# Values of two quads in one run, and their first moves issued from another queue: a cross-attention kernel on one core

## The chip, the core and the metric

One core of a Trainium2 chip. It has TensorE (PE, matmuls; its weight loads are shown as PEld), VectorE (DVE), ScalarE (ACT), GpSimd (POOL) and SyncE (SP, which here only issues DMAs). All run their own instructions in order and meet through semaphores. The metric is device time in microseconds: 567.95 is the median of three runs before the change (567.91 to 568.03).

## The reference, cut to what matters

Eight batches, each of 256 query rows `x` and 256 context rows `ctx`, 1024 wide, 32 heads of 32, all in float32:

```python
xn   = layernorm(x) * ln_gamma + ln_beta
Q    = split_heads(xn @ Wq.T)              # 8 x 32 heads x 256 x 32
K = V = split_heads(ctx)
S    = einsum('bhsd,bhtd->bhst', Q, K) * 32 ** -0.5
P    = softmax(where(mask, S, -inf))
attn = merge_heads(einsum('bhst,bhtd->bhsd', P, V))
out  = x + attn @ Wout.T
```

## The kernel before

**Quads and slots.** Four heads make a quad; a batch has NQ = 8 quads, so N = 64 quads in all. The main loop at the end of the kernel writes one slot for each `n` from 0 to 63. In a slot PE gets, in this order: `scores(n + 1)` (L486), output steps of place 0, `values(n - 2)` (L636), output steps of place 1, one query product of a coming batch (`query_product`, L447, in seven of eight slots), and, after the softmax has been written, output steps of place 2 (`product_steps`, L720). The other engines get `softmax(n + 1)` in the same slot. The order of every engine is this program order; no scheduler changes it, and semaphores are placed by what is read and written. Slots are named below by n modulo 8, slot 0 to slot 7 of a batch.

**Scores** of a quad are four heads side by side, each on 32 of PE's rows; their PSUM tiles `sc` have four buffers. **Values** work on tiles of 64 rows by 32 columns: 32 matmuls of the source, 64 records in the profile, into two PSUM tiles `pv` with two buffers. `copy_at` (ACT, L649) takes them to `at`. It is written inside the next softmax, after the first head's exponentials, so `pv` is free again well before the next values.

**Softmax** of a quad, head by head: DVE adds the mask and takes the minimum (L524), ACT takes the exponential with its sum (L528), DVE the reciprocal (`rden`, L535), POOL scales (L543), DVE transposes in blocks of 32 x 32 (L549) into `pT`, and ACT copies the second half of each pair of heads aside into `pc` (`aside`, L555). On ACT there are so eight exponentials, the first copy aside, copies of a query product (L457) in some slots, and the second copy aside, the last piece of a slot. Two of eight slots have on ACT after that a normalization of rows of `x` (L248), for slots 2 and 3. On DVE, additions of query products (L463 in slot 0, L468 in slots 5 and 6) stand between the third and the fourth transpose.

**Moves.** The blocks have to change partitions before values can read them. The tail of a quad's softmax does it with four DMAs of 128 KB, all on SP's queue: two first moves from `pT` to `pT` (L614), the loads of the slot (keys, values, rows of `x`), and two second moves from `pc` to `pT` (L618), which overwrite what the first moves have read and so wait for their landing. `values(n - 2)` reads a quad's `pT` three slots after its scores were written.

**Query products** of the next batch are seven products of quarter size (a Strassen scheme, S1, S4, A11, S2, S3, A22, A12 in slots 2 to 7 and 0), all in one PSUM bank; each one's result must be taken out before the next is begun or added to. The scores of the next batch begin in slot 7; their second half reads what S3's addition (L468, slot 6) leaves in `qa`. **Output products** are 28 steps (two records each) for each batch, spread over the slots of the next by the table `STEPS`, whose triples are the steps of places 0, 1 and 2.

Of the kernel before, what the change touches and what calls it, by code (L numbers as in the profile page):

```python
# [46 lines left out]
F32 = mybir.dt.float32  # L47
# [4 lines left out]
P = 128  # L52
# [7 lines left out]
def xattn_kernel(  # L60
# [10 lines left out]
    nc = tc.nc  # L71
# [4 lines left out]
    NQ = NC  # L76
    NH = P // HD
    NS = S // P
    NT = T // P
    NO = D // 512  # L80
    K = 32
# [4 lines left out]
    N = B * NQ  # L86
# [16 lines left out]
    ps_v = ctx.enter_context(tc.tile_pool(name="ps_v", bufs=2, space=PS))  # L103
# [367 lines left out]
    mbs, scs, pTs, pvs, ats, pos = {}, {}, {}, {}, {}, {}  # L471
# [19 lines left out]
    def softmax(*args):  # L491
        for _ in softmax_parts(*args):
            pass
# [2 lines left out]
    BY_ACT = range(1, 2 * NQ)  # L496
    BY_DVE = range(NQ, 2 * NQ)


    def softmax_parts(n, copies=(), ahead=(), between=(), hooks={}, fill=()):  # L500

        fill = list(fill)

        def fill_in():
            if fill:
                fill.pop(0)()  # L510

        pss = scs[n]
        pT = pTs[n] = ptp.tile([P, 2, NI, NH, NS, K], F32, tag="pT", name=f"pT_{n}")
        pc = asp.tile([P, NI, NH, NS, K], F32, tag="pc", name=f"pc_{n}")
        es, mns, dens = {}, {}, {}

        def exps(j, part=range(NS)):
            if 0 in part:
                es[j] = ep.tile([P, NS, T], F32, tag="e", name=f"e_{n}_{j}")
                mns[j] = sm.tile([P, NS], F32, tag="mn", name=f"mn_{n}_{j}")  # L520
                dens[j] = sm.tile([P, NS], F32, tag="den", name=f"den_{n}_{j}")
            e, mn, den = es[j], mns[j], dens[j]
            for s in part:
                nc.vector.tensor_tensor_reduce(  # L524
                    out=e[:, s, :], in0=pss[j][:, s, :], in1=mbs[n // NQ], scale=1.0,
                    scalar=NO_SCORE, op0=ALU.add, op1=ALU.min, accum_out=mn[:, s : s + 1],
                )
                nc.scalar.activation(  # L528
                    e[:, s, :], e[:, s, :], AF.Exp, bias=mn[:, s : s + 1], scale=-1.0,
                    accum_out=den[:, s : s + 1],  # L530
                )

        def normalize(j):
            rden = sm.tile([P, NS], F32, tag="rden", name=f"rden_{n}_{j}")
            nc.vector.reciprocal(rden, dens[j])  # L535
            for s in range(NS):
                if j == NH - 1 and n in BY_ACT:
                    nc.scalar.activation(
                        es[j][:, s, :], es[j][:, s, :], AF.Copy, scale=rden[:, s : s + 1]
                    )  # L540
                    continue
                engine = nc.vector if j == 1 and n in BY_DVE else nc.gpsimd
                engine.tensor_scalar(  # L543
                    es[j][:, s, :], es[j][:, s, :], rden[:, s : s + 1], 1.0,
                    ALU.mult, ALU.mult,
                )

        def blocks(j):
            nc.vector.transpose(  # L549
                pT[:, :, :, j, :, :].rearrange("p a i s k -> p (a i) s k"),  # L550
                es[j].rearrange("p s (b t) -> p b s t", t=K),
            )

        def aside(j):
            nc.scalar.copy(pc[:, :, ts(j, 2)], pT[:, 1, :, ts(j, 2)])  # L555

        if n == 0:
            for j in range(NH - 1):
                exps(j, (0,))
            yield  # L560
            exps(NH - 1, (0,))
            fill_in()
            yield
            for j in range(NH):
                exps(j, (1,))
            normalize(0)
            fill_in()
        else:
            exps(0)
            while tails:  # L570
                tails.pop()()
            for done in list(pvs):
                copy_at(done)
            exps(1)
            for hook in hooks.get("soon", ()):
                hook()
            exps(2)
            normalize(0)
            exps(3)
        if n <= NQ + 1:  # L580
            for copy in copies:
                copy()
        for hook in hooks.get(0, ()):
            hook()
        normalize(1)
        fill_in()
        if n in BY_DVE:
            normalize(2)
        blocks(0)
        for hook in hooks.get(1, ()):  # L590
            hook()
        if n not in BY_DVE:
            normalize(2)
        fill_in()
        if n in BY_ACT:
            normalize(3)
        blocks(1)
        aside(0)
        if n not in BY_ACT:
            normalize(3)  # L600
        fill_in()
        blocks(2)
        while fill:
            fill_in()
        if n > NQ + 1:
            for copy in copies:
                copy()

        def tail():
            blocks(3)  # L610
            aside(1)

            for r in range(2):
                nc.sync.dma_start(pT[ts(2 * r, K), 1], pT[ts(2 * r + 1, K), 0])  # L614
            for load in between:
                load()
            for r in range(2):
                nc.sync.dma_start(pT[ts(2 * r + 1, K), 0], pc[ts(2 * r, K)])  # L618

        for load in ahead:  # L620
            load()
        if n < NQ or n > N - NQ:
            tails.append(tail)
        else:
            tail()
        yield

    def values(n):
        pvs[n] = [
            ps_v.tile([P, 2, NS, K], F32, tag="pv", name=f"pv_{n}_{r}") for r in range(2)  # L630
        ]
        pT = pTs.pop(n)
        for i in range(NI):
            for j in range(NH):
                for r in range(2):
                    nc.tensor.matmul(  # L636
                        pvs[n][r][j * HD : (j + 1) * HD],
                        vs[n - n % 2][ts(r, 2 * K), i, ds(n % 2 * P + j * HD, HD)],
                        pT[ts(r, 2 * K), :, i, j, :, :],
                        start=(i == 0), stop=(i == NI - 1),  # L640
                    )

    def copy_at(n):
        b, c = divmod(n, NQ)
        k, c = divmod(c, NK)
        if c == 0:
            ats[b, k] = atp.tile([P, NK, NS, NA, K], F32, tag="at", name=f"at_{b}_{k}")
        for r, pv in enumerate(pvs.pop(n)):
            nc.scalar.copy(  # L649
                ats[b, k][:, c, :, ts(r, 2), :], pv.rearrange("p a s k -> p s a k")  # L650
            )
# [16 lines left out]
    P1_ASIDE = (0, 1, 2, 3, 4, 5)  # L668
    STEPS = ((0, 0, 0), (0, 7, 0), (0, 1, 2), (0, 2, 2), (0, 2, 1), (0, 1, 2), (0, 0, 3), (0, 1, 2),
             (0, 2, 0))  # L670
    ENDS = ((0, 0, 2), (0, 0, 5), (0, 0, 5)) + ((0, 0, 4),) * 4 + ((0, 0, 0),)
    ENDS_TO = {2: (0, 0), 3: (0, 1), 4: (1, 1), 5: (1, 0), 6: (1, 1), 7: (0, 1)}

    def steps_of(b):
        if b == B - 2:
            return ENDS
        return STEPS

    assert all(sum(map(sum, steps_of(b))) == len(PRODUCTS) * NK for b in range(B - 1))

    def operand(b, name):
# [237 lines left out]
    for b in range(B - 1):  # L919
        done, ends = 0, b == B - 2  # L920
        for i, counts in enumerate(steps_of(b)):
            n = NQ * (b + 1) + i
            for place, k in enumerate(counts):
                steps.setdefault((n, place), []).append((b, range(done, done + k)))
                done += k
        for i, *what in (
            ((2, keep_p1), (3, take_po_q), *((i, copy_po, i) for i in range(3, 8))) if ends else
            ((1, keep_p1), *(((2, add_p1, 0, 0),) if b else ()), (2, store, 0, 0), (3, take, 0, 1), (4, take, 1, 1), (6, store, 1, 0),
             (7, store, 1, 1), (8, store, 0, 1))
        ):  # L930
            evacuations[NQ * (b + 1) + i].append((what[0], b, *what[1:]))
# [6 lines left out]
    for n in range(N):  # L938
        b, i = divmod(n - NQ, NQ)
        new_q = new_qs[n]  # L940
        between = []
# [5 lines left out]
        if n + 3 in firsts or n + 2 in firsts:  # L947
            between, ahead = between + ahead, []
# [18 lines left out]
        for what, one, *args in evacuations[n]:  # L967
            if one == B - 2:
                now.append(partial(what, one, *args))
            else:  # L970
                place = 0 if i in (3, 4, 6) or i < 3 and what is not add_p1 else "soon" if i == 2 else 1
                hooks.setdefault(place, []).append(partial(what, one, *args))
        if n >= 2:
            values(n - 2)
        project_steps(n, 1)
        copies = [partial(copy_q, q) for q in new_q]
# [105 lines left out]
    for c in range(2):  # L1082
        end_steps(to_c11, "A12", B21, (c,), (0,))
        end_steps(to_c21, "A22", T4, (c,), (0,))
    values(N - 2)
    copy_at(N - 2)
    end_sum(slice(2, 3), nc.gpsimd)
# [3 lines left out]
    s2t2 = ps_o.tile([P, 512], F32, tag="po", name="po_end_s2")  # L1091
    end_steps(s2t2, "S2", T2, range(2), (0,))
    values(N - 1)
    copy_at(N - 1)
    end_sum(slice(3, 4), nc.vector)
# [67 lines left out]
```

## Time and profile before

| what | before |
|---|---|
| median of three runs | 567.95 us (567.91 to 568.03) |
| span of the profiled execution | 566.0 us |
| around the span, to the median | 1.95 us |
| PE busy | 561.4 us, 99% |
| DVE, ACT, POOL busy | 467.6, 423.4, 394.3 us |
| granted TensorE clock | 1.000 over the span |
| eight slots from 292.31 us on | 67.93 us |
| DMA | 119.02 MB, 210 GB/s in the mean |

The time of the profiled execution is known only by its span, from first to last instruction; the runs' times hold a little more around it. A row of the order of time gives start and length in microseconds, engine and line, what is written and read, and how many equal instructions follow each other; a bracket behind it is idle time of that engine just before and what ended it. Rows of SPq and ACTq are DMA issues of these engines' sequencers. PE's matmuls overlap, so a run's length reaches over the next one's start; start to start is what it costs.

### The profile page before, as it was taken

The numbers are of one execution on the slowest core, as the hardware profiler recorded it, in microseconds if no ns is written. First come the engines' busy times: TensorE is split into PE (matmuls) and PEld (weight loads), VectorE is DVE, ScalarE is ACT, GpSimd is POOL, SyncE is SP. The second block draws the span as 40 slices with busy tenths as digits, with TensorE's granted clock in tenths as the row PEclk, the third lists the DMA queues.
The fourth block names the chain that finished last, engine by engine and source line by source line (L and its number), as shares of the span: only waits on it lengthen the run. The fifth ranks groups of instructions, "written<-read, shape, count | busy, mean of one in ns | idle before, by whom it ended". The sixth has DMA issues, their size and how long they took to land.

```text
span 566.0 us, 20200 instructions
## 1 busy us (share of the span) xinstructions
PE 561.4 (99%) x7266; PEld 393.7 (70%) x7266; DVE 467.6 (83%) x1716; ACT 423.4 (75%) x1464; POOL 394.3 (70%) x636
## 2 busy tenths in 40 slices
PE   8999999999999999999999999999999999999997
PEld 8788886767766767667766776667766767755454
DVE  5889889999988988878898888988888777879923
ACT  4699999997778866786777876778776776769820
POOL 2788887899777656857568665777648657448780
PEclk9999999999999999999999999999999999999999
DMA  8966667856697777966778767796658864536751
GB/s 310 397 181 199 185 198 228 281 162 179 212 301 232 223 202 235 263 195 191 233 216 239 215 176 221 230 273 193 176 140 269 255 191 128 146 110 180 218 156 74
DMA packets 47219, 119.02 MB, mean 210 GB/s; under 512 B 8976, under 2 KB 9744, under 8 KB 47120
## 3 DMA queue, kind: packets, MB, share of 16 engines
q1 hardware_dynamic: 46976, 117.74, 69.5%
q8 instruction: 57, 0.93, 0.8%
q14 instruction: 42, 0.34, 0.2%
q10 hardware_dynamic: 144, 0.01, 0.0%
HBM read 66.33 MB, written 11.53 MB: 138 GB/s over the span
## 4 chain that ended last, share of the span: by engine, by line
PE 97%; DMA 1%; DVE 0%; POOL 0%; ACT 0%; issue 0%; SPq 0%; POOLq 0%
PE po_S L720 21%; PE pq_A L447 19%; PE pv L636 12%; PE sc L486 12%; PE po_A L720 11%; PE pq L345 9%; PE pq_S L447 8%; PE po_end L787 3%; PE po_last L787 1%; DMA x<-in_x_dram 1%; PE po_end_s L787 0%; POOL x L885 0%; PE pq L290 0%; PE px L307 0%; ACT e L528 0%; PE px L273 0%
## 5 line engine op out<-in xcount | busy, mean ns | idle before, releaser
L543 POOL TENSOR_SCALAR e<-e,rden 128x256 f32<-128x256 f32 x466 | 215.4, 479 | 125.5 <-DVE rden L535 123.0
L528 ACT ACTIVATE e<-e,mn 128x256 f32<-128x256 f32 x512 | 254.0, 502 | 46.1 <-DVE mn L524 44.9
L549 DVE STREAM_TRANSPOSE pT<-e 128x512 f32<-128x512 f32 x256 | 178.9, 703 | 35.6 <-POOL e L543 27.5
L524 DVE CUSTOM_DVE_ANT_0 e<-sc,mb 128x256 f32<-128x256 f32 x512 | 185.3, 415 | 25.4 <-PE sc L486 25.1
L555 ACT COPY pc<-pT 128x512 f32<-128x512 f32 x128 | 79.0, 617 | 55.7 <-DVE pT L549 35.6
L528 ACT ACTIVATION_READ_ACCUMULATOR e<-e,mn 128x1 f32 x512 | 98.4, 192 | 0.0
L486 PEld LDWEIGHTS sc<-k,qa 32*128 32x128 f32 x1024 | 46.1, 184 | 42.2 <-issue 21.6
L720 PE MATMUL po_S<-wo,at 128*128 128x512 f32 x152 | 74.3, 606 | 0.0
L636 PE MATMUL pv<-pT,v 64*32 64x128 f32 x4096 | 74.1, 274 | 0.0
L486 PE MATMUL sc<-k,qa 32*128 32x256 f32 x1024 | 73.6, 401 | 0.1
L636 PEld LDWEIGHTS pv<-pT,v 64*32 64x32 f32 x4096 | 57.0, 105 | 22.5 <-issue 11.8
L720 PE MATMUL po_A<-wo,at 128*128 128x512 f32 x128 | 59.4, 605 | 0.0
L345 PE MATMUL pq<-xnT,wq 128*128 128x256 f32 (+1 forms) x240 | 55.0, 384 | 0.0
L447 PEld LDWEIGHTS pq_A<-xnT,wq 128*128 128x128 f32 x416 | 48.5, 192 | 6.2 <-issue 4.8
L345 PEld LDWEIGHTS pq<-xnT,wq 128*128 128x128 f32 x240 | 44.6, 190 | 8.2 <-issue 1.5
L720 PE MATMUL po_S<-wo,s 128*128 128x512 f32 x104 | 50.1, 606 | 0.0
L447 PE MATMUL pq_A<-xnT,wq 128*128 128x128 f32 x416 | 48.5, 275 | 0.0
L535 DVE RECIPROCAL rden<-den 128x2 f32<-128x2 f32 x256 | 38.2, 150 | 7.3 <-ACT e L528 6.2
L524 DVE DVE_READ_ACCUMULATOR2_ANT mn<- 128x1 f32 x512 | 42.4, 83 | 0.0
L720 PEld LDWEIGHTS po_A<-wo,at 128*128 128x128 f32 x128 | 22.9, 189 | 25.6 <-issue 24.5
L720 PEld LDWEIGHTS po_S<-wo,at 128*128 128x128 f32 x152 | 25.5, 190 | 19.5 <-issue 19.5
L753 POOL TENSOR_TENSOR r<-r,p 128x512 f32<-128x512 f32 x24 | 30.6, 1277 | 4.8 <-ACT e L528 3.0
(102 smaller groups left out, 666.1 us busy)
## 6 DMA issues: line engine op xcount, KB each, us to landing
v<-in_kv_dram SPq DMA_DIRECT2D x32, 512.0 KB, 4.2
pT<-pT SPq DMA_DIRECT2D x128, 128.0 KB, 2.9
pT<-pc SPq DMA_DIRECT2D x128, 128.0 KB, 4.0
ring<-kept_T SPq DMA_DIRECT2D x20, 512.0 KB, 5.3
k<-in_kv_dram SPq DMA_DIRECT2D x32, 256.0 KB, 4.1
x<-in_x_dram SPq DMA_DIRECT2D x15, 512.0 KB, 5.6
r<-in_x_dram SPq DMA_DIRECT2D x28, 256.0 KB, 4.5
out_dram<-r SPq DMA_DIRECT2D x28, 256.0 KB, 3.2
```

Of the source, the lines that this page charges most:

```text
L345: nc.tensor.matmul(pqs[n], wq[:, o, c, :], xnTs[b](c), start=(c == 0), stop=(c == NC - 1),)
L447: nc.tensor.matmul(pqs[b][:, o, :], w[:, c], x_[:, c], start=begins and o + c == 0, stop=c == NK - 1, skip_group_check=True,)
L486: nc.tensor.matmul(scs[n][j][:, s, :], qa[r, n % NQ, ts(s, P)], ks[n - n % 2][r, n % 2, :], start=True, stop=True,)
L524: nc.vector.tensor_tensor_reduce(out=e[:, s, :], in0=pss[j][:, s, :], in1=mbs[n // NQ], scale=1.0, scalar=NO_SCORE, op0=ALU.add, op1=ALU.m ...
L528: nc.scalar.activation(e[:, s, :], e[:, s, :], AF.Exp, bias=mn[:, s : s + 1], scale=-1.0, accum_out=den[:, s : s + 1],)
L535: nc.vector.reciprocal(rden, dens[j])
L543: engine.tensor_scalar(es[j][:, s, :], es[j][:, s, :], rden[:, s : s + 1], 1.0, ALU.mult, ALU.mult,)
L549: nc.vector.transpose(pT[:, :, :, j, :, :].rearrange("p a i s k -> p (a i) s k"), es[j].rearrange("p s (b t) -> p b s t", t=K),)
L555: nc.scalar.copy(pc[:, :, ts(j, 2)], pT[:, 1, :, ts(j, 2)])
L636: nc.tensor.matmul(pvs[n][r][j * HD : (j + 1) * HD], vs[n - n % 2][ts(r, 2 * K), i, ds(n % 2 * P + j * HD, HD)], pT[ts(r, 2 * K), :, i, j, ...
L720: nc.tensor.matmul(po, operand(b, name)[:, c], wo[:, which, c], start=begins and c == 0, stop=c == NK - 1, skip_group_check=not begins,)
L753: nc.gpsimd.tensor_tensor(r, r, p1s[b], ALU.add)
```

## The change

In the even slots 16 to 56 (`PAIRED`), `values(n - 2, (n - 1,))` does two quads in one run, quad n - 2 as before and quad n - 1 one slot sooner than before; odd slots in that range have no values. A `pv` tile holds both quads, twice the size, in the same two buffers.

For quads 14 to 55 (`SOONER`) the two first moves are issued by ACT, behind the second copy aside, and the slot's loads are issued behind the second moves, which stay on SP.

For the batches whose output products fall in that range (`EVEN_STEPS`), steps are regrouped: 7, 2, 5, 2, 4, 2, 4 and 2 in slots 1 to 7 and 0 of the next batch, where 7, 3, 4, 3, 3, 3, 3 and 2 stood.

```diff
+    PAIRED = range(2 * NQ, N - NQ + 2)
+    SOONER = range(PAIRED[0] - 2, PAIRED[-1] - 1)
...
+            queue = nc.scalar if n in SOONER else nc.sync
             for r in range(2):
-                nc.sync.dma_start(pT[ts(2 * r, K), 1], pT[ts(2 * r + 1, K), 0])
-            for load in between:
-                load()
+                queue.dma_start(pT[ts(2 * r, K), 1], pT[ts(2 * r + 1, K), 0])
+            if n not in SOONER:
+                for load in between:
+                    load()
             for r in range(2):
                 nc.sync.dma_start(pT[ts(2 * r + 1, K), 0], pc[ts(2 * r, K)])
+            if n in SOONER:
+                for load in between:
+                    load()
...
-    def values(n):
-        pvs[n] = [
-            ps_v.tile([P, 2, NS, K], F32, tag="pv", name=f"pv_{n}_{r}") for r in range(2)
-        ]
+    def values(n, also=()):
+        both = [
+            ps_v.tile([P, 1 + len(also), 2, NS, K], F32, tag="pv", name=f"pv_{n}_{r}")
+            for r in range(2)
+        ]
+        for u, one in enumerate((n, *also)):
+            pvs[one] = [pv[:, u] for pv in both]
+            one_quad(one)
+
+    def one_quad(n):
         pT = pTs.pop(n)
...
+    EVEN_STEPS = ((0, 0, 0), (0, 7, 0), (0, 1, 1), (0, 3, 2), (0, 2, 0), (0, 2, 2), (0, 0, 2),
+                  (0, 2, 2), (0, 2, 0))
...
-        return STEPS
+        return EVEN_STEPS if NQ * (b + 1) in PAIRED else STEPS
...
-        if n >= 2:
+        if n in PAIRED and n % 2 == 0:
+            values(n - 2, (n - 1,))
+        elif n >= 2 and n not in PAIRED:
             values(n - 2)
```

## The prediction

> **What bounds the kernel now.** I read the page first, then the order of time of TensorE (PE), then ScalarE (ACT) and VectorE (DVE), then the queue of SyncE (SP). The page says that PE is the bound: it is busy 99% of the span, and 97% of the chain that ended last is PE.
>
> ```profile
> span 566.0 us, 20200 instructions
> PE 561.4 (99%) x7266; PEld 393.7 (70%) x7266; DVE 467.6 (83%) x1716; ACT 423.4 (75%) x1464; POOL 394.3 (70%) x636
> PE 97%; DMA 1%; DVE 0%; POOL 0%; ACT 0%; issue 0%; SPq 0%; POOLq 0%
> L636 PE MATMUL pv<-pT,v 64*32 64x128 f32 x4096 | 74.1, 274 | 0.0
> ```
>
> With no idle time on PE, an edit can gain only inside what counts as busy, where one kind of matmul follows another. PE in order of time (a matmul of the source is two records):
>
> ```profile
> 22.52 1.15 PE L486 MATMUL sc<-k,qa 32*128 32x256 f32 x16
> 23.60 3.75 PE L345 MATMUL pq<-xnT,wq 128*128 128x257 f32 x16
> ...
> 250.63 1.15 PE L486 MATMUL sc<-k,qa 32*128 32x256 f32 x16
> 251.70 1.16 PE L636 MATMUL pv<-pT,v 64*32 64x128 f32 x64
> 252.79 1.99 PE L720 MATMUL po_S<-wo,at 128*128 128x512 f32 x4
> 254.61 3.73 PE L447 MATMUL pq_A<-xnT,ring 128*128 128x128 f32 x32
> 258.18 1.02 PE L720 MATMUL po_S<-wo,at 128*128 128x512 f32 x2
> 259.13 1.15 PE L486 MATMUL sc<-k,qa 32*128 32x256 f32 x16
> ...
> 288.64 3.73 PE L447 MATMUL pq_A<-xnT,wq 128*128 128x128 f32 x32
> 292.31 1.15 PE L486 MATMUL sc<-k,qa 32*128 32x256 f32 x16
> ...
> 294.47 6.28 PE L720 MATMUL po_A<-wo,at 128*128 128x512 f32 x14
> 300.68 1.15 PE L486 MATMUL sc<-k,qa 32*128 32x256 f32 x16
> ```
>
> Start to start, this gives the units of a slot: scores 1.08, values 1.09, a query product 3.57 (3.67 before scores, 288.64 to 292.31), output steps 0.96 for one (two records), 1.82 for two, so 2.68 for three, and 6.21 for seven. A batch of eight slots is one window:
>
> ```profile
> 292.31:360.24 67.93, 67.93 (x922) 48.05 (x921) 58.09 (x213) 51.40 (x179) 45.99 (x81) 1.00 0.74 207
> ```
>
> The columns are PE, PEld, DVE, ACT, POOL busy, then clock. PE is busy for all 67.93 us at clock 1.00, and ACT for 51.40. ACT has room by this count; whether it has room in its order is the question below.
>
> **The gain on PE.** A run of values ends 1.16 us after its first start, and its last record takes 0.27, so that one starts at 0.89; the next kind starts at 1.09, 0.20 after it. Inside the run a record follows each 0.89/63 = 0.014. Leaving the run thus costs 0.20 - 0.014 = 0.185 us. Two quads in one run leave it once: 0.185 saved for each pair. Nothing of that comes back in the odd slot: scores followed by a full-array matmul take 1.08 (22.52 to 23.60) as before values. Pairs stand at even slots 16 to 56: 21 x 0.185 = 3.9 us. The regrouped output steps are 28 as before.
>
> By the units the slots of a batch become (n modulo 8; even ones hold 1.08 + 1.09 + 0.90 = 3.07 of scores and values): slot 0 8.56, slot 1 7.29, slot 2 8.55, slot 3 9.14, slot 4 8.56, slot 5 8.28, slot 6 8.55, slot 7 8.28, together 67.2 where 67.93 stood.
>
> **The price on ACT.** SP's issues stand here as the trace has them, with ACT around them, and the one DMA that ACT issues now:
>
> ```profile
> 1.00 0.38 ACTq L193 DMA_DIRECT2D gb<-in_gamma_beta_dram  x1
> ...
> 259.40 0.63 ACT L555 COPY pc<-pT 128x512 f32<-128x512 f32 x1
> 260.05 1.15 SPq L614 DMA_DIRECT2D pT<-pT  x2
> 260.85 0.51 ACT L528 ACTIVATE e<-e,mn 128x256 f32<-128x256 f32 x1 [0.82 <-DVE mn L524]
> 261.25 0.58 SPq L135 DMA_DIRECT2D k<-in_kv_dram  x1
> ...
> 263.60 1.14 SPq L618 DMA_DIRECT2D pT<-pc  x2
> ```
>
> The two first moves keep SP 1.2 us (260.05 to 261.25). On ACT they stand between the second copy aside, whose end they wait for, and the next slot's first exponential: 42 slots x 1.2 us. In the slot shown ACT idled 0.82 there. To see how far such holes carry, take a slot in which ACT came late by itself, since it had normalized rows of x first (L248):
>
> ```profile
> 378.69 1.24 ACT L248 ACTIVATE x<-x,shift,rstd 128x1024 f32<-128x1024 f32 x1
> 379.83 0.49 ACT L528 ACTIVATE e<-e,mn 128x256 f32<-128x256 f32 x1
> 380.81 0.40 ACT L649 COPY at<-pv 128x128 f32<-128x128 f32 x2
> 382.68 2.82 POOL L543 TENSOR_SCALAR e<-e,rden 128x256 f32<-128x256 f32 x6 [0.47 <-DVE rden L535]
> 383.59 0.50 ACT L528 ACTIVATE e<-e,mn 128x256 f32<-128x256 f32 x1
> 384.28 0.12 DVE L535 RECIPROCAL rden<-den 128x2 f32<-128x2 f32 x1
> 384.55 0.71 DVE L549 STREAM_TRANSPOSE pT<-e 128x512 f32<-128x512 f32 x1
> 386.28 0.62 ACT L555 COPY pc<-pT 128x512 f32<-128x512 f32 x1 [0.23 <-DVE pT L549]
> ```
>
> From the first exponential (379.83) through the last (383.59), GpSimd's normalizing, DVE's transposes and the copy aside (end 386.90) go 7.07 us, each step waiting for the one before: the loop that ACT cannot shorten, since the next exponentials are queued behind the copy. Four copies of values instead of two lengthen an even slot by about 0.3, none shortens an odd one by as much. With the issues the loop is 7.07 + 1.2 = 8.27 a slot, plus twice 1.24 a batch for L248: 68.6, above PE's 67.2. So ACT falls behind PE within a batch. Where PE meets it again:
>
> ```profile
> 274.43 0.71 DVE L549 STREAM_TRANSPOSE pT<-e 128x512 f32<-128x512 f32 x1
> 275.06 0.65 DVE L468 TENSOR_TENSOR qa<-pq_A,qa 128x512 f32<-128x512 f32 x1
> ...
> 292.42 0.69 DVE L463 TENSOR_TENSOR qa<-pq_A,xnT 128x512 f32<-128x512 f32 x1
> 293.03 0.70 DVE L549 STREAM_TRANSPOSE pT<-e 128x512 f32<-128x512 f32 x1
> 293.76 0.62 ACT L555 COPY pc<-pT 128x512 f32<-128x512 f32 x1 [1.60 <-DVE pT L549]
> ```
>
> In slot 0 the last query product ends as slot 1's scores begin (292.31); its add (L463), the last transpose and the copy aside end 2.07 later (294.38): PE sets ACT's time there. In slot 6 the add of product S3 (L468) stands on DVE behind the third transpose, and the second half of the next slot's scores, 0.41 after the first half, reads its result. The chain from slot 1's start to the end of that add: 2.07, six times 1.2 for issues, five slots of 7.07 = 35.35, two L248 = 2.48, and in slot 6 4.72 to the third transpose (379.83 to 384.55) + 0.3 + 0.63 + 0.65 = 6.30. Sum 53.40. PE comes there after slots 1 to 6, 50.37, + 0.41 = 50.78. PE waits 2.6 us in each batch with both L248 in its slots (those from slots 16, 24, 32, 40), and 0.1 in that from 48, which has none. Without the issues the chain is 46.2, so that nothing of it shows today. The first moves also wait on ACT for the landing of the DMA that last used their semaphore, mostly a second move of the slot before that is some microseconds old; I cost this at nothing, and L248 and the exponentials queued behind would pay each microsecond of it.
>
> **The issue's price** is the term that decides. No row shows this transfer issued by ACT. Nearest is the same transfer on SP, above; from below the 0.38 of ACT's own small one; from above SP's median:
>
> ```profile
> L614 SPq DMA_DIRECT2D pT<-pT x128: 507/582/2155, 26.0 to 540.8; - x128
> L618 SPq DMA_DIRECT2D pT<-pc x128: 507/513/1651, 33.5 to 543.2; - x128
> DMA to landing us min/median/max: 2.2/4.0/7.0
> ```
>
> I take 0.6 each with the gap, since the transfer is the same. At 0.507 each (1.06 a slot) the wait is 2.64 - 6 x 0.14 = 1.8; at 0.38 (0.81) it is 0.3; at 0.65 (1.3), an estimate from SP's median and 0.07 of gaps, it is 3.2.
>
> **The other parts.** SP gives up 1.2 us a slot. Second moves (L618) issue as the first land and no longer behind a load's 0.58; loads start about one landing later but are used one to three slots (over 8 us) after, so I cost them at nothing; if a load came late, PE would wait the difference. The second quad of a pair is read at 8.56 + 8.28 + 1.98 = 18.8 us after its scores start (17.8 from slot 0, since slot 1 is short). From slot 0 the copy aside ends at 8.56 + 2.07 = 10.6; two issues of 0.6 and two landings (last row above, that of L618) give 16.2 at the least landing, 2.2, and 19.8 at the median, 4.0. PE then waits up to 2.0 at values in slot 2. That costs nothing further as long as the 2.6 later in the batch covers it, since ACT's chain doesn't wait for it. Without that cover it would be the price. In PSUM pv doubles inside its two buffers; its copies end most of a slot before the next pair.
>
> The Trainium skill ("DMA: Bandwidth & Descriptors", section "Issuing engines are not separate DMA queues") says that issuing from several engines saves only sequencer time, "usually small relative to the DMA itself". By it the moves land no sooner from ACT, which my sum doesn't count on; if small meant near nothing, the wait would vanish and the first rival below holds; the trace's issue rows speak against that.
>
> **Sum.** The profiled span is 566.0; the median of the runs is 567.95, 1.95 more for what lies around it. -3.9 + 4 x 2.64 + 0.1 = +6.8: span 572.8, time 574.7.
>
> **Rivals.** (1) ACT pays little for an issue, and the chain stays under PE's: the gain remains. With 0.38 each: -3.9 + 4 x 0.3 = -2.7, 565.2; with no wait at all 564.0. For it speak ACT's row of 0.38 and its 51.40 busy of 67.93; against it that every row of SP with this transfer is at least 0.507. It decides below 0.46 each, where 4 waits equal 3.9. (2) Waits and gain cancel: an issue of about 0.46, 567 to 569. (3) The moved quad also comes late: landings at the median in slot 2, where the cover fails. Landings up to 7.0 speak for it, SP's shorter queue ahead of the second moves against it. About 1.5 us for each of five batches above the forecast: 582.
>
> **How the numbers follow.** Forecast 0.60, (1) 0.27, (2) 0.06, (3) 0.07. The forecast's own range is 570 to 577.5 (issues of 0.507 to 0.65). The range takes in (1) and reaches from 564.3 to 577.5. Faster and slower count from 0.2%, 1.1 us, about what a measurement can tell: faster 0.27, same 0.06, slower 0.67.
>
> **What would show it.** Values of 128 records in even slots and the saving at their end; ACTq rows of about 0.57 behind each copy aside; first exponentials 3 us after scores in slot 1, over 5 in slots 4 to 6; the wait of scores in slot 7 for L468, up to 2.6 us, in four batches (part of it earlier in slot 6, where S1 opens its bank behind L762 of DVE). The forecast is wrong if ACTq rows are short, if exponentials start by 2 us in every slot, or if PE waits for pT instead.

## The result, and the profile after

The changed kernel takes 603.12 us (599.25 to 611.71, six runs), the one before 567.99 in the same session (567.86 to 568.34, six runs): ratio 1.0602, 95% interval 1.0575 to 1.0629. Medians here and below are over all runs; ratios and intervals leave out a run more than 1.5% above the fastest of its kernel (one of six here), so a median can sit a little beside its ratio. It is slower, as forecast, but by 35 us and not by 7, and outside the range. The profiled execution took 602.83 (span 601.0).

From the page of the changed kernel, the busy times, the granted clock in 40 slices, and the shares of the chain that ended last (the lines moved: scores L486, values L650, output steps L736, first moves L618, second moves L623, DVE's additions to the output rows r, which empty the bank of the output steps, L774 and L778, exponentials L531):

```profile
span 601.0 us, 20158 instructions
...
PE 571.5 (95%) x7266; PEld 399.5 (66%) x7266; DVE 473.7 (79%) x1716; ACT 424.9 (71%) x1464; POOL 394.4 (66%) x636
...
PEclk9999999999999999999999999999999989999999
...
PE 53%; DMA 14%; POOL 9%; ACT 7%; DVE 7%; issue 4%; ACTq 3%; SPq 2%; DVEq 0%; POOLq 0%
```

PE's share of the chain fell from 97% to 53%; the rest goes in turn over DMA, POOL, ACT and DVE. The work itself is the same. PE's idle time grew from 4.6 us (566.0 - 561.4) to 29.5 (601.0 - 571.5), and the list of waits names most of it (engine, line, what it waited for: total, times, longest; PEld and PE rows of one line can be the same wait, seen by the weight load and by the matmul, so they are not added):

```profile
PEld po_S L736 <- DVE r L778: 11.3, 11, 1.9
...
PE pv L650 <- DMA pT<-pc: 9.7, 10, 2.3
PE po_S L736 <- DVE r L778: 9.2, 9, 1.7
...
PE po_S L736 <- DVE r L774: 3.7, 4, 1.3
...
PEld sc L486 <- DVE qa L468: 3.5, 5, 1.5
```

PE's busy time is 10.1 us longer too, for the same matmuls. Two stretches at half clock, of 3.41 us each (one is in the last section), are some 3.4 of it; the rest is not explained here.

One batch in order of time on PE, and the same batch as a window (columns as in the prediction), 73.83 us where 67.93 stood:

```profile
317.98 2.11 PE L650 MATMUL pv<-pT,v 64*32 64x128 f32 x128
320.01 1.12 PE L736 MATMUL po_A<-wo,at 128*128 128x512 f32 x2
...
334.08 1.98 PE L736 MATMUL po_S<-wo,at 128*128 128x512 f32 x4 [0.81 <-DVE r L774]
336.00 1.15 PE L486 MATMUL sc<-k,qa 32*128 32x256 f32 x16
337.07 1.16 PE L650 MATMUL pv<-pT,v 64*32 64x128 f32 x64
339.56 0.38 PE L650 MATMUL pv<-pT,v 64*32 64x128 f32 x2 [1.32 <-DMA pT<-pc]
340.71 1.14 PE L650 MATMUL pv<-pT,v 64*32 64x128 f32 x62 [0.78 <-DMA pT<-pc]
...
372.81 1.98 PE L736 MATMUL po_S<-wo,at 128*128 128x512 f32 x4 [1.69 <-DVE r L778]
```
```profile
309.62:383.45 73.83, 69.21 (x922) 48.85 (x921) 59.37 (x212) 51.63 (x179) 46.05 (x81) 1.00 0.69 201
```

Three things are to be seen. A run of 128 costs 2.03 from its start to the next kind where nothing holds it (317.98 to 320.01; 2.05 in the run c_pair46 below); two runs of 64 cost 2 x 1.09 = 2.18, so a pair saves about 0.135. In slot 4 PE stands twice between the two quads of a pair, for second moves (2.1 us of idle time); over the whole run its waits at values are 5.4 us in slot 4, 2.7 in slot 6 and 1.6 in slot 2. In slots 3 and 7 the output steps wait for DVE's additions that empty their bank, which come late; that late exponentials on ACT make them late is argued here, and the experiments bear on it. In the batch shown these waits don't cover each other: they follow one another.

### The profile page after: what moved, and what is told of

It is laid out like the page before. It is cut to its first block, busy times and chain, and to the rows that moved or that the text cites. A ratio compares the mean times of both kernels' runs of the same rounds, so it can differ in the third digit from the quotient of the medians.

```text
span 601.0 us, 20158 instructions
## 1 busy us (share of the span) xinstructions
PE 571.5 (95%) x7266; PEld 399.5 (66%) x7266; DVE 473.7 (79%) x1716; ACT 424.9 (71%) x1464; POOL 394.4 (66%) x636
## 4 chain that ended last, share of the span: by engine, by line
PE 53%; DMA 14%; POOL 9%; ACT 7%; DVE 7%; issue 4%; ACTq 3%; SPq 2%; DVEq 0%; POOLq 0%
PE po_S L736 10%; PE pq_A L447 10%; PE pq L345 9%; POOL e L546 8%; PE pv L650 7%; PE sc L486 6%; PE po_A L736 4%; ACT e L531 4%; DMA r<-in_x_dram 4%; DMA pT<-pT 3%; DVE pT L552 3%; PE po_end L803 3%; ACTq L618 3%; DMA pT<-pc 2%; DVE e L527 2%
## 5 line engine op out<-in xcount | busy, mean ns | idle before, releaser
L531 ACT ACTIVATE e<-e,mn 128x256 f32<-128x256 f32 x512 | 253.7, 502 | 63.4 <-DVE mn L527 45.2
L531 ACT ACTIVATION_READ_ACCUMULATOR e<-e,mn 128x1 f32 x512 | 99.0, 193 | 0.0
L650 PE MATMUL pv<-pT,v 64*32 64x128 f32 x4096 | 75.6, 278 | 10.0 <-DMA pT<-pc 9.7
L736 PE MATMUL po_S<-wo,at 128*128 128x512 f32 x152 | 74.9, 615 | 9.2 <-DVE r L778 5.5
L650 PEld LDWEIGHTS pv<-pT,v 64*32 64x32 f32 x4096 | 60.3, 107 | 28.9 <-issue 20.4
L486 PE MATMUL sc<-k,qa 32*128 32x256 f32 x1024 | 75.0, 402 | 1.6 <-DVE qa L468 1.5
L486 PEld LDWEIGHTS sc<-k,qa 32*128 32x128 f32 x1024 | 45.6, 184 | 42.4 <-issue 19.3
L736 PE MATMUL po_A<-wo,at 128*128 128x512 f32 x128 | 59.4, 605 | 0.0
L736 PE MATMUL po_S<-wo,s 128*128 128x512 f32 x104 | 50.7, 611 | 3.7 <-DVE r L778 3.6
L736 PEld LDWEIGHTS po_S<-wo,at 128*128 128x128 f32 x152 | 26.1, 191 | 34.0 <-issue 21.4
L736 PEld LDWEIGHTS po_A<-wo,at 128*128 128x128 f32 x128 | 22.9, 189 | 26.5 <-issue 24.2
```

The costliest lines, as they stand in the source:

```text
L486: nc.tensor.matmul(scs[n][j][:, s, :], qa[r, n % NQ, ts(s, P)], ks[n - n % 2][r, n % 2, :], start=True, stop=True,)
L531: nc.scalar.activation(e[:, s, :], e[:, s, :], AF.Exp, bias=mn[:, s : s + 1], scale=-1.0, accum_out=den[:, s : s + 1],)
L650: nc.tensor.matmul(pvs[n][r][j * HD : (j + 1) * HD], vs[n - n % 2][ts(r, 2 * K), i, ds(n % 2 * P + j * HD, HD)], pT[ts(r, 2 * K), :, i, j, ...
L736: nc.tensor.matmul(po, operand(b, name)[:, c], wo[:, which, c], start=begins and c == 0, stop=c == NK - 1, skip_group_check=not begins,)
```

## The experiments

### One part at a time, and two at a time

The change has three parts: pairs (with the regrouped steps), first moves issued by ACT, loads behind the second moves. Each part alone is the kernel before with these lines:

```diff
# a_act
-                nc.sync.dma_start(pT[ts(2 * r, K), 1], pT[ts(2 * r + 1, K), 0])
+                queue.dma_start(pT[ts(2 * r, K), 1], pT[ts(2 * r + 1, K), 0])
# a_behind: "for load in between" behind the second moves, for quads in SOONER
# a_pair
+        if n in PAIRED and n % 2 == 0:
+            values(n - 2, (n - 1,))
+        return EVEN_STEPS if NQ * (b + 1) in PAIRED else STEPS
```

> Only the first moves go to ScalarE; values and loads stay as before. Theory ISSUE (the forecast's own: 1.2 us a slot in ACT's in-order loop, which reaches PE only at the second half of the scores in slot 7): no 3.9 us gain, a wait of about 2 to 2.6 us in four batches, so 574 to 579 us. Theory PAIR (the missing 28 us come from the second quad of a pair, read a slot sooner): nothing of them here, 568 to 579 us, and PE never waits at values. Theory LANDING (first moves and ACT's waits for shared completions are what grew): over 585 us, with waits at values or holes over 2 us on ACT in most slots.

> Only the loads go behind the second moves; issue and values stay as before. Theories ISSUE and PAIR: hidden, 567 to 569 us. Theory LOADS (a load behind the second moves waits on SP for the landing of the first moves, so the rows of x for the output, r, come late): 572 to 585 us, with GpSimd's add to r waiting for a DMA in slots 18 and 50 as in the changed kernel (5 us there).

> Values in pairs with the regrouped output steps, moves on SP and loads in between as before. Theory ISSUE: the gain of 3.9 us, less what the second quad is late, 564 to 569 us. Theory PAIR: PE waits at values for the second quad in most even slots, 1 to 3 us in 21 pairs, 575 to 600 us. If SP's moves without ACT make the chain of exponentials short again, scores in slot 7 don't wait for L468.

> The changed kernel with the first moves back on SP. Theory ISSUE (ACT's issue is what costs): 564 to 570 us. Theory LOADS: 575 to 590 us, r late. Theory PAIR: 570 to 595 us, though less than with loads in between, since second moves then issue 0.6 us sooner.

Of two parts together, a_pair_behind leaves out the issue on ACT, b_pair_act the loads' new place, b_act_behind the pairs:

> Pairs and issue on ACT, loads in between as before. Theory ADD (each part has its own waits, and they add): 568 + 28 + 16 = 612 us. Theory CHAIN (there is one chain of exponentials, moves and stores, and what is late in one part hides what is late in another): 595 to 602 us, near issue on ACT by itself less the 3.9 us of gain.

> Issue on ACT and loads behind the second moves, values one by one. Theory ADD: 568 + 28 + 41 = 637 us. Theory CHAIN: 595 to 608 us, since SP without the first moves gets to the loads earlier, and PE's waits for the ring in slot 2 are gone as they are in the changed kernel.

| parts | time, us (runs) | over before | ratio, 95% interval |
|---|---|---|---|
| issue on ACT | 596.61 (4) | 28 | 1.0497 [1.0473, 1.0521] |
| loads behind | 609.19 (4) | 41 | 1.0715 [1.0667, 1.0763] |
| pairs | 583.91 (4) | 16 | 1.0274 [1.0218, 1.0331] |
| pairs, loads behind | 610.06 (4) | 42 | 1.0733 [1.0703, 1.0763] |
| pairs, issue on ACT | 603.10 (4) | 35 | 1.0597 [1.0573, 1.0622] |
| issue on ACT, loads behind | 599.18 (4) | 31 | 1.0484 [1.0431, 1.0536] |
| all three (the change) | 603.12 (6) | 35 | 1.0602 [1.0575, 1.0629] |

Every part loses by itself, and the losses don't add up: 28, 41 and 16 would be 85. The loads alone (609.19, at most 585 expected) and pairs with the loads (610.06, at most 595) lie above every range given for them. The theory ADD fell (612 and 637 expected); CHAIN is near (595 to 602 for pairs with the issue, 603.10 came; 595 to 608 for the issue with the loads, 599.18). Given the issue on ACT, pairs add 6.5 (603.10 - 596.61) and the loads' place nothing that these intervals tell (603.12 against 603.10 with pairs; 599.18 against 596.61 without). The first of these two equalities hides unequal clocks: the mean granted clock was 0.983 to 0.989 in the runs with pairs and the issue, 0.989 to 0.994 in the changed kernel's (its run at 611.71 left out), an estimated 9 and 5 us (1 minus the clock, times the span).

### The issue on ACT: time, or waiting

Here the kernel before gets only the time on ACT, no transfer. The copies repeat part of the copy aside onto itself, so nothing is left out:

```diff
                 nc.sync.dma_start(pT[ts(2 * r, K), 1], pT[ts(2 * r + 1, K), 0])
+            if n in SOONER:
+                for _ in range(2):
+                    nc.scalar.copy(pc[:, :, ts(1, 2)], pc[:, :, ts(1, 2)])
```

> The kernel before, with two copies of the second half of the copy aside onto itself on ACT behind the second copy aside, in the 42 slots (2 x 0.62 us by the rows of that copy): ACT loses the 1.2 us a slot that the forecast put down for two issues, but waits for no DMA. Theory ISSUE (the 1.2 us alone make the 28 us that issue on ACT cost by itself): 590 to 600 us. Theory LANDING (most of the 28 us are ACT's waits for the landing of transfers that used the same completion before, up to 4.5 us each in the run with issue alone): 572 to 580 us, as the forecast's chain has it.

577.69 us, ratio 1.0164 [1.0125, 1.0202], 9.3 us over its before. ACT's order of time, PE's in slot 6 of a batch (output steps L735, additions L777 here), and the batch as a window:

```profile
299.20 0.62 ACT L558 COPY pc<-pT 128x512 f32<-128x512 f32 x1 [1.48 <-DVE pT L552]
299.85 1.27 ACT L621 COPY pc<-pc 128x512 f32<-128x512 f32 x2
301.03 0.50 ACT L531 ACTIVATE e<-e,mn 128x256 f32<-128x256 f32 x1
```
```profile
347.84 2.84 PE L735 MATMUL po_S<-wo,s 128*128 128x512 f32 x6 [1.12 <-DVE r L777]
```
```profile
297.06:367.28 70.22, 68.92 (x922) 48.15 (x921) 58.74 (x214) 60.94 (x195) 46.24 (x81) 1.00 0.70 204
```

The hole behind the copy aside is 1.21 us (299.82 to 301.03), as put in, and the batch is 2.29 longer, 70.22 against 67.93. Four such batches make 9.2: the forecast's chain, 2.64 for each of four batches and 10.7 in all, measured without its gain. PE meets it mostly in slot 6, at the bank that DVE's addition empties, one place earlier than the scores of slot 7. So theory ISSUE holds for 9 of the 28 us, and 19 need another cause. The way to PE is the same: its waits for that addition, in b_act_nop and in the run with the issue alone, are

```profile
PE po_S L735 <- DVE r L777: 4.5, 4, 1.1
...
PE po_S L732 <- DVE r L774: 20.3, 13, 3.3
```

With the real issue, an early slot shows a part of it (ACT and SP in the run with the issue alone):

```profile
141.48 4.64 SPq L332 DMA_DIRECT2D xnT<-xe  x6
...
141.67 0.62 ACT L558 COPY pc<-pT 128x512 f32<-128x512 f32 x1 [0.98 <-DVE pT L552]
...
143.25 3.44 ACTq L618 DMA_DIRECT2D pT<-pT  x2
...
146.22 0.53 SPq L402 DMA_DIRECT2D kept_T<-ring  x1
...
146.80 0.51 ACT L531 ACTIVATE e<-e,mn 128x256 f32<-128x256 f32 x1 [4.51 <-DMA xnT<-xe]
```

An exponential reads nothing of `xnT`. But in the program as built the DMAs of both queues use eight completion semaphores in turn (553 DMAs in this trace, 69 or 70 on each), and an issue waits until the last transfer on its semaphore has landed. Here the second of the two first moves follows, eight DMAs later, one of the moves of x that SP was issuing: that one was issued at 142.74 and landed at 146.16, ACT's issue began at 146.18, and ACT stood 4.5 us where 1.2 is the mere issue. From the list of waits of the same run (each holds the 1.2 of the issues too):

```profile
ACT e L531 <- DMA pT<-pT: 13.2, 5, 3.2
...
ACT e L531 <- DMA xnT<-xe: 4.5, 1, 4.5
...
ACT e L531 <- DMA out_dram<-r: 2.7, 1, 2.7
```

To tell waiting from an issue that is dear everywhere, the issue was given to ACT in a part of the slots:

```diff
# d_act_mid; d_act_edge has "not in"
-            queue = nc.scalar if n in SOONER else nc.sync
+            queue = nc.scalar if n in SOONER and n % NQ in range(2, 7) else nc.sync
```

> Issue on ACT alone, but only for the first moves of quads 2 to 6 of each batch (26 of the 42); those of quads 7, 0 and 1, whose issue waits for a move of x or a load in the run with all on ACT, stay on SP. Theory LANDING (ACT's waits for completions shared with SP's transfers make the 19 us between issue on ACT and the same time spent on ACT without a transfer): five of six issues of the forecast's chain are left, 2.64 - 1.2 = 1.4 us in each of four batches, 574 us, and 572 to 580. Theory ISSUE-LONG (an issue on ACT simply costs more than its row shows, in each slot alike): 26/42 of 28 us, 583 to 588.

> The complement: on ACT only the first moves of quads 7, 0 and 1 (16 of 42). Theory LANDING with one chain: the waits of 2 to 4 us are there, but the chain without the other five issues is 46.2 + 1.2 + these against 50.8 of PE, so most is absorbed, 568 to 575 us. Theory ISSUE-LONG: 16/42 of 28 us, 577 to 581.

Middle quads: 582.06 us (4 runs), ratio 1.0233 [1.0207, 1.0260], 13.5 over; edge quads: 575.36 (4), 1.0118 [1.0103, 1.0132], 6.8 over. Both lie just above the range that LANDING gave and just below that of ISSUE-LONG, so the times alone don't decide. The sum of both is 20 of 28. In the edge run the exponentials wait as named:

```profile
ACT e L531 <- DMA xnT<-xe: 8.0, 4, 2.9
...
ACT e L531 <- DMA out_dram<-r: 5.3, 3, 2.3
...
ACT e L531 <- DMA pT<-pT: 4.3, 2, 2.2
```

and the issue is no longer than forecast (all 32 there, nanoseconds: least, median, most):

```profile
L618 ACTq DMA_DIRECT2D pT<-pT x32: 514/515/1374, 141.3 to 488.3; - x32
```

That speaks against an issue that is dear everywhere. (With the middle quads 6 of 52 issues took over 1 us, the longest 1.59.) In the run with the middle quads a new wait came up, which neither theory had: GpSimd for late rows r, and DVE behind it.

```profile
DVE r L774 <- POOL r L765: 10.0, 6, 4.0
...
POOL r L765 <- DMA r<-in_x_dram: 9.2, 3, 4.9
```

The traces also give the whole of it on ACT. From the end of each second copy aside to the end of the second issue is 1.2 us in the median, about 0.54 for each issue and 0.12 of gaps. What goes beyond, in microseconds over all slots:

| first moves issued by ACT | beyond 1.2 a slot | of it waiting | of it issues over 0.54 each |
|---|---|---|---|
| all 42 quads (a_act) | 20.3 | 14.0 | 6.2 |
| 26 middle quads (d_act_mid) | 7.5 | 1.3 | 6.2 |
| 16 edge quads (d_act_edge) | 8.4 | 7.8 | 0.6 |
| all 42, the changed kernel | 8.7 | 3.9 | 4.7 |

In a_act it is in few slots: 12 of 42 hold over 1.6 us, and in 9 of these an issue waited 0.5 us or more until a transfer of SP, eight DMAs before it, had landed (five times a move of x, twice a load of the ring, twice a second move; the list of waits above infers the names of transfers and has other ones for some).

So the waits for landings at the issue are shown, and where they stand; with the longer issues, for which no cause is shown, they are as large as the 19 us. That each microsecond of them reaches PE is not shown, and some 2 to 4 of the 28 us are a lower clock (last section). A run in which ACT issues and shares no semaphore with SP was not tried. The Trainium skill ("DMA: Bandwidth & Descriptors", section "Anatomy of one DMA — SWDGE (gpsimd) path", told there of DMAs that GpSimd issues) says that the DMA engines themselves don't wait on semaphores; the issuing sequencer does, ahead of dispatch. These rows agree: the wait stands on ACT, and ACT's exponentials behind it.

### The loads

The run with the loads alone behind the second moves, in slots 1 and 2 of a batch: SP, then PE, GpSimd and ACT:

```profile
314.73 0.57 SPq L143 DMA_DIRECT2D v<-in_kv_dram  x1
315.36 0.43 SPq L412 DMA_DIRECT2D ring<-kept_T  x1
...
316.37 1.16 SPq L618 DMA_DIRECT2D pT<-pT  x2
321.93 1.63 SPq L623 DMA_DIRECT2D pT<-pc  x2
...
324.22 0.44 SPq L412 DMA_DIRECT2D ring<-kept_T  x1
324.71 0.43 SPq L149 DMA_DIRECT2D r<-in_x_dram  x1
```
```profile
328.98 3.60 PE L447 MATMUL pq_S<-sx,ring 128*128 128x128 f32 x16 [5.46 <-DMA ring<-kept_T]
...
330.29 1.27 POOL L769 TENSOR_TENSOR r<-r,p 128x512 f32<-128x512 f32 x1 [10.13 <-DMA r<-in_x_dram]
...
331.60 0.69 DVE L778 TENSOR_TENSOR r<-po_A,r 128x512 f32<-128x512 f32 x1 [9.26 <-POOL r L769]
...
334.16 0.62 ACT L558 COPY pc<-pT 128x512 f32<-128x512 f32 x1 [9.84 <-DVE rden L538]
```

A load behind the second moves flies just ahead of the next slot's first moves. Behind two of 512 KB (314.73, 315.36) the second moves, which wait for the first ones' landing, start 5.6 us after them (316.37 to 321.93; 2.4 a slot earlier, 309.36 to 311.74), and the next loads stand behind that on SP. Before, loads flew while SP waited anyway. The second half of the ring and the first r come too late, and four engines stand: PE waits for the ring 23.1 us in the whole run, five times.

```diff
# b_keep_ring: FIRST = (load_ring,); b_keep_r: (load_res,); d_keep_both: (load_ring, load_res)
             for load in between:
-                load()
+                if n not in SOONER or load.func in FIRST:
+                    load()
...              # behind the second moves
+            for load in between:
+                if n in SOONER and load.func not in FIRST:
+                    load()
```

> Loads behind the second moves, except those of the ring (kept sums of Wq), which stay between first and second moves. Theory RING (PE's 5 us in slot 2 of each batch, waiting for the ring, are the loss): 568 to 576 us. Theory R (the rows r come late, and GpSimd, DVE and ACT stand behind one another for 9 to 10 us in slot 2): 590 us or more, with GpSimd still waiting for r up to 10 us.

> Loads behind the second moves, except the rows r, which stay between. Theory RING: 595 to 610 us, PE's waits for the ring in slot 2 still near 5 us. Theory R: 568 to 580 us, and the waits of GpSimd for r gone.

> Loads of keys, values, x and masks behind the second moves, those of the ring and of r in between. If the ring and r together are what the loads cost (each alone left 27 to 29 of the 41 us): 568 to 573 us. If it matters that any 512 KB load stands ahead of the next first moves: 580 us or more.

596.86 us with the ring kept between (ratio 1.0469 [1.0417, 1.0522]), 595.46 with r (1.0454 [1.0411, 1.0497]), 586.15 with both (1.0264 [1.0215, 1.0313]), where 609.19 stood. RING, R and the two together each fail as the one cause: each takes 12 to 14 us, both take 23 of 41, and the rest stays with the loads of keys, values, x and masks. Which of these counts was not separated. The time is in the expectation's second range, for any 512 KB load ahead of the next first moves (values are 512 KB); that this is the reason was not tested by itself. Of the 41 us some 12 are a lower clock (last section), which follows the waits.

### The pairs

In the run with pairs alone PE waits for the second quad in slots 0 and 2:

```profile
PE pv L646 <- DMA pT<-pc: 6.4, 7, 1.6
...
PE pv L646 <- DMA xnT<-xe: 3.2, 3, 1.8
```

Values read nothing of `xnT`; the profile names what landed last before. Four kernels tried what makes the second quad late. The x moves go in two lots of eight and leave slot 5 free in b_pair_fit, c_pair_fit2 and d_pair460:

```diff
-                moves=tuple(first - 6 + (i + 2) // 6 for i in range(16)),
+                moves=tuple(first - 6 + 2 * (i // 8) for i in range(16)),
# b_pair_fit besides: both halves of T1 and the first r are loaded in slot 7
-((n - 3, n - 2), "T1")
+((n - 3, n - 3), "T1")
# c_pair_fit2: second half of T1 and first r behind the second moves of slot 7; 8 steps in slot 1, 1 in slot 2
# c_pair46: pairs in slots 4 and 6 only, steps regrouped there alone, moves of x as before
# d_pair460: pairs in slots 4, 6 and 0
```

> Values in pairs, first moves on SP, loads in between, with what stood on SP ahead of the second quad's moves in slots 7 and 1 taken away: the moves of the normalized x go in two lots of eight in slots 4 and 6 (none in slot 5), both halves of the ring's T1 and the first rows r are loaded in slot 7. Theory PAIR-LATE (the 12 us that pairs cost by themselves are PE's waits at values in slots 0 and 2 because SP's queue held those moves): waits gone, the gain of 3.9 us left, 563.5 to 566 us. Theory PAIR-SOON (a slot is too short for two moves, whatever stands around them): 570 us or more, PE waits at values in other slots too.

> All 21 pairs, moves on SP, loads in between. Moves of x in lots of eight in slots 4 and 6; of what the first attempt put between the moves of slot 7, the second half of T1 and the first r now go behind the second moves; slot 1 of PE gets one output step more (8) and slot 2 one less, so that slot 1 is 0.9 us longer. Theory PAIR-LATE: waits at values under 0.5 us a batch, 564 to 567 us. If PE still waits 1 us or more in slot 2 of each batch: 569 to 580 us.

> Pairs only in slots 4 and 6 of each batch (10 pairs), where the run with pairs alone showed no wait of PE at values; moves and loads as before. Theory PAIR-LATE: 0.185 us saved ten times and no new wait, 565.8 to 567 us, 0.2 to 0.4% faster. Theory PAIR-SOON: PE waits there too, as soon as nothing else delays the slots, 568 us or more.

> Pairs in slots 4, 6 and 0 of each batch (16 pairs), one by one in slots 1 to 3; moves of x in lots of eight in slots 4 and 6, so that nothing of them stands ahead of quad 7's moves; all else as before. If slot 0 was late for the moves of x alone: 16 x 0.185 = 3.0 us gained, 564.9 to 566.5 us. If not: waits at values in slot 0 of 1 us or more, 567 us or more.

| pairs | time, us (runs) | ratio, 95% interval |
|---|---|---|
| all 21, first mending (b_pair_fit) | 594.71 (4) | 1.0463 [1.0418, 1.0508] |
| all 21, second mending (c_pair_fit2) | 584.36 (4) | 1.0265 [1.0216, 1.0315] |
| slots 4, 6, 0, x in two lots (d_pair460) | 572.54 (6) | 1.0073 [1.0047, 1.0099] |
| slots 4 and 6 (c_pair46) | 567.94 (12) | 0.9994 [0.9971, 1.0016] |

Both mendings failed by the theory's own numbers. In the first, what had been taken from the second quad's way stood in the first quad's, and slot 2 waited for both: 15.2 us at values in its profile, and by its clock of 0.980 some 12 more. In the second, 10.1 us of waits at values stayed, most of them in slot 2. With pairs in slots 4, 6 and 0 the waits at values are down to 1.3 us, and yet 4 us are lost; where they go is not shown. The smallest set of pairs is the only one that doesn't lose, and it doesn't gain what can be told from no change. A batch of it, of 67.67 us where 67.93 stood, shows why: two pairs save 2 x 0.135 = 0.27.

```profile
223.96:291.63 67.67, 67.67 (x922) 48.34 (x921) 57.98 (x213) 51.61 (x180) 45.99 (x81) 1.00 0.76 220
```

No version here beats the kernel before by more than its measurement tells.

## Why the prediction was wrong in size

- **What bounds, and the direction:** right. PE has no idle time to give, the issue makes ACT's loop longer than PE's slots, and the chain reaches PE late in each batch.
- **The issue's price:** right. 0.6 each with the gap; the changed kernel's rows (below) have 526 ns in the median, and 1.2 us of ACT's time a slot cost 9.3 us against 10.7 forecast. Only the few issues of over 1 us were not in it (4.7 us in the changed kernel). The Trainium skill's "usually small relative to the DMA itself" ("DMA: Bandwidth & Descriptors", section "Issuing engines are not separate DMA queues"), weighed in the prediction, agrees as a ratio, 0.5 us of 4.5 to the landing in the run with the issue alone; the time on ACT was not small for this kernel. PE paid it at the fallback named (output steps in slot 6 behind DVE), more than at L468.

```profile
L618 ACTq DMA_DIRECT2D pT<-pT x84: 514/526/1434, 133.5 to 517.2; - x84
```

- **"The first moves also wait on ACT for the landing of the DMA that last used their semaphore ... I cost this at nothing":** this is the step that failed. Issue on ACT alone cost 28 us where time alone cost 9. Between them ACT's trace has 14.0 us of these waits and 6.2 of longer issues. "Some microseconds old" was nearly true of the middle quads (1.3 us of waits in 26 slots) and false of quads 7, 0 and 1 (7.8 us in 16), where SP issues moves of x, six in a row in the slot shown. In the changed kernel itself the waits are 3.9 us and the longer issues 4.7; there PE also waits for the second quad, next.
- **The second quad "costs nothing further as long as the 2.6 later in the batch covers it":** failed. Lateness was foreseen, up to 2.0 in slot 2; it came mostly in slots 4 and 6, and the cover was not there: PE waits 9.7 us at values, and with the issue on ACT pairs cost 6.5 instead of giving. Rival (3), at 582 and a chance of 0.07, named this mechanism.
- **The gain:** mis-sized. 0.135 a pair, 2.8 in all, not 0.185 and 3.9. Going from one quad to the next inside a run costs 0.05 that the sum didn't have.
- **The loads "I cost them at nothing":** right beside the issue on ACT (603.12 with, 603.10 without), wrong as reasoned: by themselves they cost 41. What held was probably not the slack of one to three slots but that SP, without first moves in its queue, came to the loads earlier; no run shows this by itself. In the changed kernel PE waits for the ring 0.4 us at most.

By measured steps: 568.0 + 9.3 (time on ACT) + 19 (the rest of the issue on ACT) + 6.5 (pairs) + 0 (loads) = 602.8, against 603.12. The order of the steps is a choice, since the parts don't add, and the 19 is what the issue cost alone: inside the changed kernel less of it is waiting on ACT (8.7 us beyond 1.2 a slot, against 20.3) and more is waiting for second moves.

## What to carry to other kernels

A DMA moved to a compute engine's queue brings two prices: its issue, which the trace of another queue gives well, and its wait for a completion shared with other queues, which stands in front of that engine's next work; look up which transfer used the semaphore before and how old it will be. Before costing a moved load at nothing, see which transfer it will now fly ahead of. And don't count on one wait to cover another: here those in slots 3, 4 and 7 of one batch followed each other, though the losses of the parts, taken alone, did not add.

## What was not expected of the hardware

**The granted clock fell after a wait.** In the changed kernel a stretch of 3.41 us ran at half clock (columns as above, clock before DMA share):

```profile
281.25:284.66 3.41, 1.65 (x78) 1.13 (x80) 3.41 (x15) 0.70 (x2) 2.90 (x3) 1.00 0.50 96
284.66:288.07 3.41, 3.41 (x69) 3.03 (x70) 1.53 (x8) 2.44 (x11) 0.93 (x2) 0.50 0.67 218
```

PE was busy 1.65 of 3.41 us, waiting for second moves, and paid for it in the next 3.41. At half rate that is about 1.7 us more, so that a wait of 2 us came near to costing double. It doesn't follow each time: in the run with the loads alone a window with PE busy for 1.50 us was followed by one at full clock, in which PE stood still, and only the next (328.85 to 332.26) ran at 0.50.

```profile
322.02:325.44 3.42, 1.50 (x14) 1.31 (x12) 0.32 (x2) 2.30 (x10) 0.00 (x0) 1.00 0.49 101
325.44:328.85 3.41, 0.00 (x0) 0.00 (x0) 0.00 (x0) 0.00 (x0) 0.00 (x0) 1.00 1.00 327
```

Over a run it counts. By the mean granted clock (1 minus it, times the span; an estimate) it is 12 of the 41 us of the loads alone (0.980), 12 of the 26 of the first mending of pairs (0.980), 2 to 4 of the 28 of the issue alone (0.993 to 0.997) and none where only time was put on ACT (1.000). The Trainium skill ("TensorE: Matmul & The Clock Gate", section "Part 1: The HAM clock gate (the "warmup" mystery)") gives windows of 3413 ns in which activity sets the clock, and the half rate after an idle one; the length agrees, but here, in the changed kernel, the window before was idle by half only.

**First moves land later from ACT's queue:** 4.5 us in the median (last column, from issue to landing) of the run with the issue alone, 2.9 for the same transfer on SP in the kernel before. The 2.9 takes in the first and last batches; from 125 to 515 us, where ACT issues in the other run, SP's median is 3.4. SP's loads, which had stood behind them in one queue, can now start beside or ahead of them; that this is the cause was only argued. The rows are of the pages' list of DMA issues, of the one and of the other:

```profile
pT<-pT ACTq DMA_DIRECT2D x84, 128.0 KB, 4.5
```
```profile
pT<-pT SPq DMA_DIRECT2D x128, 128.0 KB, 2.9
```
